# Halo copies at even steps, a quarter's squares on VectorE, and masks two slots later

## The chip, the cores and the metric

The kernel runs on one core of a Trainium2 chip. The time is in device microseconds (us), from the first to the last work of one execution. A kernel's time is the median of several executions on the chip. The core has a matrix engine (TensorE, "PE" in the profile, with its weight loads as "PEld"), a vector engine (VectorE, "DVE"), a scalar engine (ScalarE, "ACT"), a general engine (GpSimd, "POOL") and an engine that here only issues DMAs (SyncE, "SP"). Each takes its instructions in the order in which the program has put them; they wait for each other through semaphores. TensorE writes its products into PSUM banks, and the others read them from there.

## The reference

Four layers on `x` of shape (1024, 16, 16, 16), that is batch, height, width and 16 channels, in float32. Each layer is `x = x + layer(gn(x))`, where `gn` is a group norm over 8 groups of two channels.

```python
def _gn(v, G=8, eps=1e-5):
    g = v.reshape(B_, H_, W_, G, C_ // G)
    m = jnp.mean(g, axis=(1, 2, 4), keepdims=True)
    s = jnp.var(g, axis=(1, 2, 4), keepdims=True)
    return ((g - m) / jnp.sqrt(s + eps)).reshape(v.shape)
...
# layers 1 and 3: a cell update, xt is x with the channels first
    pre = _alive(xt)                       # 3x3 maximum of channel 3 > 0.1
    p = jnp.concatenate([xt, y1, y2], axis=1)   # y1, y2: two 3x3 filters of each channel
    h = jax.nn.relu(flat @ fc0_w.T + fc0_b)     # 48 -> 128, for each position
    d = (h @ fc1_w.T + fc1_b)                   # 128 -> 16
    xn = (xt + d) * (pre & _alive(d))
...
# layer 2: a 3x3 convolution, 16 -> 16 channels
    out = jax.lax.conv_general_dilated(x, filters, (1, 1), 'SAME', ...) + bias
...
x = x + layer0(_gn(x))    # a product with a matrix in tensor-train form
x = x + layer1(_gn(x))    # cell update
x = x + layer2(_gn(x))    # convolution
x = x + layer3(_gn(x))    # cell update
```

## The kernel before

The batch is cut into two chunks of 512, `n` = 0 and 1; the normed input of each lies in SBUF as `X0` and `X1` (128 partitions x 32 lines x 512). While a layer works on one chunk, the other engines prepare the other chunk for the next pass: they load it, norm it, and store it. The unnormed values (`xf`) lie in DRAM.

After layer 0, which ends near 1762 us, there are six passes. This document calls them

- cell pass 1 and 2: layer 1 on chunks 0 and 1 (about 1762 to 2030 and 2030 to 2278 us),
- convolution pass 1 and 2: layer 2 on chunks 0 and 1 (2278 to 2388 and 2388 to 2492),
- cell pass 3 and 4: layer 3 on chunks 0 and 1 (2492 to 2750 and 2750 to 3018); pass 4 also turns the result into the order of the output, and a tail of DMAs ends at 3041.

*The order.* `run()` puts the steps of a pass (`main`) one after the other and weaves other work between them. Each such list `bg` comes with a span `(bg, lo, hi)`, as shares of the pass: a step of `bg` is put behind the main step at which its share is reached. In one engine's queue the order is then fixed; nothing overtakes. In cell pass 1, the work woven in first is `last`, in the span 0 to 0.18: the group norm of the last quarter of chunk 0. Then the norm of the other chunk follows.

*A norm.* For a quarter (`parts_cw`) or a whole chunk (`norm_cw`, `norm_lines`): sums over lines (L614, L622, L630 on VectorE), a matmul for the mean (L749, in `norm_lines` L717), a copy of it to SBUF by ScalarE (L678), the subtraction (L655), squares (L640 on ScalarE, or L642 on VectorE, where `on_act` is not set), the sum of the squares (L622, L630, named `s2`), a matmul for the variance (L753, L721), its root on ScalarE (L695), the reciprocal with a Newton step (L701 to L705), a matmul that spreads it (L765), and the multiplication (L655). Sums and squares have few buffers (`t4`).

*A cell pass* works on quads (four lines) in 64 turns; two quads, `v` = 0 and 1, make a column pair (q, w2), eight pairs make a quarter q. The first layer of the cell's network is a set of tile matmuls (L1495, K of 32 rows, up to four of them side by side), each sum in one of six `h` banks, which ScalarE empties with a ReLU into `hid` (L1498). The second layer, `fc1` (L1346, 8 matmuls in two halves for a pair: one for each `v`), writes `po` in one of two `o` banks. `plan()` fixes the turns beforehand: a slot is one set of tiles or one `fc1`, and there are 241 slots, six to a pair in the first quarter. With the second `fc1` of a pair comes `finish`: in the first quarter a flag of the new value (L1354), and always the update `u` (L1358, two buffers), both on VectorE. A flag of the old value (L1376) is made at a pair's first tile.

*The masks.* They depend on the position in the pair and are made in the first quarter only. The count matmuls of a pair (L1385, `pcnt`, two products, each in one of the same six `h` banks) need the flags of the pair itself and of its two neighbours; so the mask of pair w2-1 is made after pair w2 is finished, and with the quarter's last pair two masks come at once. VectorE turns the counts into a mask (L1390, L1391). Then GpSimd multiplies the update with it and adds the residual (L1397, L1398), and SP stores the result seven slots later (L1400). In pass 4 the store is replaced by `turn` eight slots later: four transposes (L1407) into an `o` bank and two copies out of it by VectorE (L159).

`later` holds what is to come at a slot; `after(n, fn)` puts `fn` n slots behind the present one. The masks of a pair are put three slots behind the second `fc1`. In the last three quarters the masks are there already, and GpSimd's two steps follow the update at once.

*A convolution pass* goes over 16 lines h in pairs. Seven steps make a pair of lines: for each line two steps of inner products (L1222, two matmuls a step), one step with the products across quarters (L1231) for both lines, and a last inner step for each line. An `o` bank is emptied by ScalarE (L1270), and GpSimd issues a DMA that adds it to `xf` in DRAM (L1271). L1231 reads lines that lie in other partitions; they are copied beforehand into `hx` by ScalarE, eight small copies (L1210) for four lines, which stand in the list `pending`. Each step takes one of them off the list, so they go out in the first eight steps after `pending` was filled, which happens every 14 steps.

Of the kernel before, what the change touches and what calls it, by code (L numbers as in the profile page):

```python
# [103 lines left out]
def conv_preact_kernel(ctx: ExitStack, tc: tile.TileContext, a: dict, out: bass.AP):  # L104
# [498 lines left out]
    def line_sum(parts, name, own, dear=False):  # L603

        st = {}

        def first():
            if own:  # L610
                st["t"], st["q"] = parts[0](), parts[1]()
                return add(1)()
            st["t"] = work([P, 2, NB], "t4", name)
            V.tensor_tensor(st["t"], parts[0](), parts[1](), ALU.add)  # L614

        def add(i):
            def go():
                x = st["q"] if own else parts[i]()
                if own and not dear and i + 1 < len(parts):

                    st["q"] = parts[i + 1]()
                V.tensor_tensor(st["t"], st["t"], x, ALU.add)  # L622
                if own and dear and i + 1 < len(parts):
                    st["q"] = parts[i + 1]()

            return go

        def last():
            st["s"] = work([P, NB], "s", name + "s")
            V.tensor_tensor(st["s"], st["t"][:, 0], st["t"][:, 1], ALU.add)  # L630

        x = 1.2 if dear else 0.0
        return st, [(1.2 + 2 * x, first)] + [(1.2 + x, add(i)) for i in range(2, len(parts))] + [(0.8, last)]
# [95 lines left out]
        steps += [5, var, 2, keep] + rstd(st)  # L729
        return steps + by_rows(each(X, 0, NL, lambda: st["r"], ALU.mult))  # L730

    def parts_cw(X, on_act):

        st = {}
        N = defaultdict(list)
        for q in range(4):
            l0 = 8 * q
            parts = [lambda l=l: X[:, l : l + 2] for l in range(l0, l0 + 8, 2)]
            s1, more1 = line_sum(parts, "s1", False)
            s2, more2 = line_sum(squares(X, l0, 8, on_act), "s2", True, not on_act)  # L740
            N["sums"].append(more1)
            N["sq"].append(
                centred(each(X, l0, 8, lambda q=q: st["m", q], ALU.subtract), more2)
            )
            rows = slice(32 * q, 32 * q + 32)

            def mean_q(s1=s1):
                st["p"] = psum([P, NB], "pmean")
                T.matmul(st["p"], gm_cw, s1["s"], start=True, stop=True)  # L749

            def var_q(rows=rows, s2=s2):
                st["v"] = psum([P, NB], "pvar")
                T.matmul(  # L753
                    st["v"][rows], gv_cw.rearrange("p f j -> p (f j)"), s2["s"],
                    start=True, stop=True,
                )

            def keep_q(rows=rows):
                if "ve" not in st:
                    st["ve"] = work([P, NB], "n", "ve")  # L760
                V.tensor_scalar(st["ve"][rows], st["v"][rows], GN_EPS, None, ALU.add)

            def spread_q(rows=rows):
                st["p"] = psum([P, NB], "pr")
                T.matmul(st["p"], sel[rows], st["r"][rows], start=True, stop=True)  # L765

            N["mean"].append(mean_q)
            N["var"].append(var_q)
            N["keep"].append(keep_q)
            N["held"].append(held(st, q))  # L770
            N["spread"].append(spread_q)
            N["mul"].append(each(X, l0, 8, lambda q=q: st["m", q], ALU.mult))
        return st, N
# [416 lines left out]
    def layer_conv(X, n, other):  # L1190

        st = {}
        pending = []

        def halo(k):

            steps = []

            def begin():
                st["h", k] = work([P, 2, 2, NB], "hx", "hx")
                if k == 0:
                    G.memset(st["h", k][0:32, :, 0], 0.0)

            def copy(b, wh):
                ls = [l for l in (4 * k - 1 + b, 4 * k + 1 + b) if 0 <= l < S]
                at = (ls[0] - (4 * k - 1 + b)) // 2
                l0 = 16 * (1 - wh) + ls[0]
                A.copy(  # L1210
                    st["h", k][32 * b : 32 * b + 32, wh, at : at + len(ls)],
                    X[96 * wh : 96 * wh + 32, l0 : l0 + 2 * len(ls) - 1 : 2],
                )

            def piece(b, wh):
                return lambda: ((b, wh) == (0, 0) and begin(), copy(b, wh))

            return [piece(b, wh) for b in range(4) for wh in range(2)]

        def inner(h, y):  # L1220
            for wh in range(2):
                T.matmul(  # L1222
                    st["po", h][wh], conv["fw"][:, y], X[:, 16 * wh + h + y - 1],
                    start=y == max(0, 1 - h), stop=y == min(2, S - h),
                )

        def across(h):
            rows = slice(0, 96 if h >= S - 2 else P)
            for wh in range(2):
                cols = slice(0, 32) if wh else slice(96, 128)  # L1230
                T.matmul(  # L1231
                    st["po", h][wh][cols], conv["hw"][rows, wh, h % 2],
                    st["h", h // 4][rows, wh, h // 2 % 2], start=False, stop=False,
                )

        def first(h):
            if h % 4 == 0 and h + 4 < S:
                pending.extend(halo(h // 4 + 1))
            st["po", h] = [bank([P, NB], "o", "po2") for _ in range(2)]
            inner(h, max(0, 1 - h))  # L1240
            if h % 2 == 0 and h > 0:
                finish(h - 2)

        def middle(h):
            inner(h, 1)
            if h % 2 == 0 and h > 0:
                finish(h - 1)

        def last(h):
            inner(h, min(2, S - h))  # L1250
            if h == S - 1:
                finish(h - 1)
                finish(h)

        def step(*fs):
            def go():
                for f in fs:
                    f()
                if pending:
                    pending.pop(0)()  # L1260

            return go

        def finish(h):

            if h == 0:
                G.tensor_copy(come, other[0:1, NL - 1, 0:1])
            for wh in range(2):
                r = work([P, NB], "r", "conv")
                A.activation(r, st["po", h][wh], AF.Identity, bias=b2)  # L1270
                G.dma_start(rows_wc(xf[2][n], wh, h), r.unsqueeze(1), accum_op=ALU.add)  # L1271

        steps = []
        for h in range(0, S, 2):
            for j in (h, h + 1):
                steps.append(step(lambda j=j: first(j)))
                if 0 < j < S - 1:
                    steps.append(step(lambda j=j: middle(j)))
            steps += [
                step(lambda h=h: across(h), lambda h=h: across(h + 1)),  # L1280
                step(lambda h=h: last(h)), step(lambda h=h: last(h + 1)),
            ]
        return halo(0), steps

    def layer_nca(X, n, l, L, xo=None):


        st = {}
# [63 lines left out]
        def finish(q, w2, po):  # L1352
            if q == 0:
                V.tensor_scalar(  # L1354
                    st["f", w2][64:96], po[96:128], nca["b1"][96:128], ALIVE, ALU.add, ALU.is_gt
                )
            u = st["u", q, w2] = work([P, NB], "u", "u")
            V.scalar_tensor_tensor(u, po, nca["b1"], X[:, 8 * q + w2], ALU.add, ALU.add)  # L1358
            if q > 0:
                residual(q, w2)  # L1360
                return

            ws = range(w2 - 1 if w2 else 0, 8 if w2 == 7 else w2)

            def masked():
                for w in ws:
                    mask(w)
                    residual(0, w)

            for w in ws:  # L1370
                fetch(w)
            after(3, masked)

        def flags(w2):
            f = st["f", w2] = work([P, NB], "f", "flags", BF16)
# [166 lines left out]
    X0, X1 = XN  # L1542
# [18 lines left out]
    with ExitStack() as es:  # L1561
# [42 lines left out]
        for i in (2, 3):  # L1604
# [1 line left out]
                steps_of(phases[i]), 415, (), (part_steps(i), 0.05, 0.9),  # L1606
                ([lambda: conv.update(s=conv_weights()), 60, lambda: conv["s"]()] if i == 2 else [0.0], 0.0, 0.5),
            )
        nst, N = parts_cw(X0, True)
        for q in range(4):  # L1610
            bg = alone(N, q - 1) if q else [0.0]
            if q == 3:
# [21 lines left out]
    with ExitStack() as es:  # L1634
        shared[0] = "m"
        stage(es, conv_sb, conv_ps)
        (first0, main0), (first1, main1) = layer_conv(X0, 0, X1), layer_conv(X1, 1, X0)
        bg = norm_lines(X1)

        bg = bg[:-16] + woven(bg[-16:], *[(6 + i, copy) for i, copy in enumerate(first1)])  # L1640
        run((lambda: now(first0), main0), 108, load_wc(X1, xf[2][1]), (bg, 0.09, 1.04), by=0.07)
        run(
            (lambda: None, main1), 108, load_cw(X0, xf[3][0]) + [put(L3)], (norm_cw(X0, True), 0.09, 1.06), by=0.07
        )
    with ExitStack() as es:
        shared[0] = "o"
# [41 lines left out]
```

## Time and profile before

| | |
|---|---|
| time, median of 3 runs | 3043.16 us (3041.85 to 3044.43) |
| the profiled execution | 3042.73 us, span 3041.0 us, mean granted TensorE clock 0.989 |
| TensorE busy in cell pass 1 (1762 to 2030) | 262.50 of 268.00 us, clock 0.99 |
| cell pass 2 (2030 to 2278) | 247.25 of 248.00 us, clock 0.99 |
| convolution pass 1 (2278 to 2388) | 106.54 of 110.00 us, clock 0.98 |
| convolution pass 2 (2388 to 2492) | 99.92 of 104.00 us, clock 1.00 |
| cell pass 3 (2492 to 2750) | 255.68 of 258.00 us, clock 0.99 |
| cell pass 4 (2750 to 3018) | 264.10 of 268.00 us, clock 1.00 |

The span is the time from the first to the last instruction in the trace; the execution's own time is 1.73 us longer. Most of the kernel (up to 1762 us) is layer 0, which the change does not reach except for one argument that is evaluated there. How to read it: in every pass TensorE is busy for nearly all of the time, so what matters are single gaps, and whether TensorE ran at full clock behind them. A groups line of the profile gives the code line, the engine, the operation, the tiles (out<-in), the shape, the count, then the busy time and the mean of one, then the idle time ahead of it and what ended that. A line of the timeline gives the start, the length, the engine, the code line, the operation, the tiles, the shape and the count of instructions taken together; in brackets, the idle time ahead of it and whose end released it.

### The profile page before, as it was taken

The numbers are of one execution on the slowest core, as the hardware profiler recorded it, in microseconds if no ns is written. First come the engines' busy times: TensorE is split into PE (matmuls) and PEld (weight loads), VectorE is DVE, ScalarE is ACT, GpSimd is POOL, SyncE is SP. The second block draws the span as 40 slices with busy tenths as digits, with TensorE's granted clock in tenths as the row PEclk, the third lists the DMA queues.
The fourth block names the chain that finished last, engine by engine and source line by source line (L and its number), as shares of the span: only waits on it lengthen the run. The fifth ranks groups of instructions, "written<-read, shape, count | busy, mean of one in ns | idle before, by whom it ended". The sixth has DMA issues, their size and how long they took to land.

```text
span 3041.0 us, 36525 instructions
## 1 busy us (share of the span) xinstructions
PE 2971.9 (98%) x13690; PEld 1239.6 (41%) x13690; DVE 1761.4 (58%) x2340; ACT 1099.3 (36%) x1806; POOL 671.6 (22%) x729
## 2 busy tenths in 40 slices
PE   7999999999999999999999999999999999999996
PEld 5544334444444444444444433333333333333332
DVE  5354337555554555544555668756977766856432
ACT  4431441000000000000101156666667656666563
POOL 1124670200000000000000015434542224432331
PEclk8999999999999999999999999999999999999998
DMA  8543664533334333332222235436437866343555
GB/s 310 225 126 99 147 150 151 166 109 109 109 109 149 124 109 109 109 102 88 88 88 94 71 131 167 137 119 204 124 121 183 193 109 199 123 127 110 155 158 197
DMA packets 251520, 418.37 MB, mean 138 GB/s; under 512 B 34868, under 2 KB 105064, under 8 KB 248272
## 3 DMA queue, kind: packets, MB, share of 16 engines
q1 hardware_dynamic: 225776, 362.53, 36.6%
q0 software_dynamic: 25376, 53.38, 8.5%
q8 instruction: 108, 1.77, 0.2%
q14 instruction: 68, 0.56, 0.1%
q10 hardware_dynamic: 192, 0.13, 0.0%
HBM read 238.58 MB, written 165.53 MB: 133 GB/s over the span
## 4 chain that ended last, share of the span: by engine, by line
PE 88%; issue 4%; POOL 2%; DVE 2%; DMA 2%; ACT 1%; SPq 0%; POOLq 0%; DVEq 0%; ACTq 0%
PE po L1134 51%; PE ph L1495 20%; PE po L1346 7%; PE pw L1057 3%; PE po L1222 2%; POOL xf L1271 1%; PE L_conv_pe L392 1%; PE ptin L866 1%; DVE bn L860 1%; POOL res L1398 1%; PE ptx L1407 1%; POOL u L1397 1%; PE po L1231 0%; ACT hx L1210 0%; DMA gq<-g_dram 0%
## 5 line engine op out<-in xcount | busy, mean ns | idle before, releaser
L1134 PE MATMUL po<-xn,w 128*128 128x512 f32 x3584 | 1575.6, 596 | 0.8 <-DVE xn L946 0.8
L1134 PEld LDWEIGHTS po<-xn,w 128*128 128x128 f32 x3584 | 670.8, 190 | 839.8 <-issue 820.9
L1498 ACT ACTIVATE hid<-ph,pack 128x512 f32<-128x512 f32 x1024 | 652.7, 686 | 381.5 <-PE ph L1495 271.6
L1170 DVE TENSOR_TENSOR r<-r,po 128x512 f32<-128x512 f32 x576 | 377.9, 684 | 577.5 <-PE po L1134 525.0
L1397 POOL TENSOR_TENSOR u<-u,mask 128x512 f32<-128x512 f32 x124 | 193.9, 1564 | 1820.9 <-DVE mask L1391 1404.2
L1062 ACT COPY w<-pw 128x512 f32<-128x512 f32 (+1 forms) x320 | 150.6, 557 | 1212.1 <-issue 1006.4
L1495 PE MATMUL ph<-xn,wq 32*128 32x512 f32 x3664 | 567.1, 611 | 0.0
L1495 PEld LDWEIGHTS ph<-xn,wq 32*128 32x128 f32 x3664 | 233.3, 184 | 270.0 <-issue 237.6
L1495 PE MATMUL ph<-xn,pack 32*128 32x512 f32 x1288 | 298.8, 625 | 4.9 <-ACT hid L1498 3.0
L1346 PE MATMUL po<-hid,pack 128*32 128x512 f32 x2048 | 281.7, 607 | 0.0
L1075 DVE TENSOR_TENSOR w<-w 128x512 f32<-128x512 f32 x320 | 210.9, 686 | 90.6 <-ACT w L1062 90.6
L655 DVE TENSOR_TENSOR xn<-xn,m 128x1024 f32<-128x1024 f32 x160 | 216.2, 1382 | 45.0 <-ACT m L678 44.8
L1358 DVE SCALAR_TENSOR_TENSOR u<-po,pack,xn 128x512 f32<-128x512 f32 x128 | 95.8, 749 | 203.3 <-PE po L1346 197.0
L1398 POOL TENSOR_TENSOR res<-res,u 128x512 f32<-128x512 f32 x124 | 206.5, 1666 | 9.7
L1222 PE MATMUL po<-xn,convw 128*128 128x512 f32 x368 | 166.2, 604 | 2.9 <-ACT conv L1270 2.9
L1495 PEld LDWEIGHTS ph<-xn,pack 32*128 32x128 f32 x1288 | 115.0, 185 | 104.3 <-issue 63.9
L1170 DVE TENSOR_TENSOR xn<-xn,po 128x512 f32<-128x512 f32 x96 | 64.4, 684 | 123.7 <-PE po L1134 123.3
L1346 PEld LDWEIGHTS po<-hid,pack 128*32 128x32 f32 x2048 | 42.8, 108 | 195.2 <-issue 144.3
L622 DVE TENSOR_TENSOR sq<-sq 128x1024 f32<-128x1024 f32 x78 | 109.8, 1407 | 13.3 <-ACT sq L640 12.6
L1222 PEld LDWEIGHTS po<-xn,convw 128*128 128x128 f32 x368 | 68.7, 191 | 99.7 <-issue 90.4
L404 POOL DMA_DIRECT2D L_conv_wy<-xn x160 | 88.8, 563 | 26.8 <-ACT xn L398 15.6
L1057 PE MATMUL pw<-R,gq 32*128 32x256 f32 (+1 forms) x1280 | 89.3, 384 | 2.9 <-DMA gq<-g_dram 2.8
(166 smaller groups left out, 1769.2 us busy)
## 6 DMA issues: line engine op xcount, KB each, us to landing
xf<-r SPq DMA_DIRECT2D x112, 512.0 KB, 3.8
xn<-xf SPq DMA_DIRECT2D x96, 512.0 KB, 4.9
r<-xf SPq DMA_DIRECT2D x80, 512.0 KB, 4.6
wq<-L_conv_wy SPq DMA_DIRECT2D x192, 192.0 KB, 2.8
res<-xf SPq DMA_DIRECT2D x128, 256.0 KB, 3.2
xf<-res SPq DMA_DIRECT2D x96, 256.0 KB, 2.1
res<-xr SPq DMA_DIRECT2D x256, 64.0 KB, 2.8
xf<-conv POOLq DMA_DIRECT2D x64, 256.0 KB, 5.7
```

The source lines that it names most:

```text
L655: V.tensor_tensor(part, part, m().unsqueeze(1).broadcast_to([P, 2, NB]), op)
L1057: T.matmul(pw[r][:, v], st["g", u][rows, v], st["R"][rows, p % 2, 64 * k0 : 256], start=True, stop=True,)
L1062: A.copy(w[:, k0:4, :, 32 * r : 32 * r + 32].rearrange("p k t (v o) -> p v (k t) o", v=2), pw[r],)
L1075: V.tensor_tensor(w[:, k], w[:, x], w[:, y], ALU.add if sign > 0 else ALU.subtract)
L1134: T.matmul(po, st["w", u][:, matrix, t], x, start=t == 0, stop=t == 3)
L1170: V.tensor_tensor(r[at], r[at], po, ALU.add if sign > 0 else ALU.subtract)
L1222: T.matmul(st["po", h][wh], conv["fw"][:, y], X[:, 16 * wh + h + y - 1], start=y == max(0, 1 - h), stop=y == min(2, S - h),)
L1346: T.matmul(po[32 * j : 32 * j + 32], nca["w1"][:, v], hid[j], start=v == 0, stop=v == 1)
L1397: by.tensor_tensor(u, u, st["m"][:, w2], ALU.mult)
L1398: by.tensor_tensor(r, r, u, ALU.add)
L1495: T.matmul(ph, w, x, start=k == 0, stop=k == len(tiles) - 1)
L1498: A.activation(h, ph, AF.Relu, bias=nca["bt"][:, r : r + 1])
```

## The change

There are four edits.

1. `parts_cw` gets an argument `alone_from`. From this quarter on, squares are made by VectorE (L642) and not by ScalarE (L640), with the order of buffers that goes with it. For chunk 0 ahead of cell pass 1 it is 3: the last quarter's four squares, which stand in `last`.
2. In `layer_conv`, the steps count themselves, and a halo copy is taken off the list only when the count modulo 7 is even: at four steps of seven, so eight copies go out in 14 steps and not in eight.
3. In the cell passes the masks of a pair come five slots behind the second `fc1`, not three. With them move the count matmuls, GpSimd's two steps, and what is put seven or eight slots behind these (stores, in pass 4 transposes). This holds for the first quarter of all four cell passes.
4. In convolution pass 2 the norm of chunk 0 for layer 3 starts at 0.12 of the pass, not at 0.09.

```diff
-    def parts_cw(X, on_act):
+    def parts_cw(X, on_act, alone_from=4):
...
-            s2, more2 = line_sum(squares(X, l0, 8, on_act), "s2", True, not on_act)
+            act = on_act and q < alone_from
+            s2, more2 = line_sum(squares(X, l0, 8, act), "s2", True, not act)
...
                 for f in fs:
                     f()
-                if pending:
+
+                st["n"] = st.get("n", 0) + 1
+                if pending and st["n"] % 7 % 2 == 0:
                     pending.pop(0)()
...
             for w in ws:
                 fetch(w)
-            after(3, masked)
+            after(5, masked)
...
-        nst, N = parts_cw(X0, True)
+        nst, N = parts_cw(X0, True, 3)
...
-            (lambda: None, main1), 108, load_cw(X0, xf[3][0]) + [put(L3)], (norm_cw(X0, True), 0.09, 1.06), by=0.07
+            (lambda: None, main1), 108, load_cw(X0, xf[3][0]) + [put(L3)], (norm_cw(X0, True), 0.12, 1.06), by=0.07
```

## The prediction

> **What bounds the kernel now.** I read the page first, then the windows (busy time and granted clock in stretches), then the timeline of each engine where TensorE is not full, and last the built instruction order of both kernels, which carries no times. The names of passes and steps are those of the section on the kernel.
>
> ```profile
> PE 2971.9 (98%) x13690; PEld 1239.6 (41%) x13690; DVE 1761.4 (58%) x2340; ACT 1099.3 (36%) x1806; POOL 671.6 (22%) x729
> PE 88%; issue 4%; POOL 2%; DVE 2%; DMA 2%; ACT 1%; SPq 0%; POOLq 0%; DVEq 0%; ACTq 0%
> ```
>
> TensorE sets the end: 98% busy and 88% of the chain. What is left over is small and local, so an edit is worth what it does to TensorE's order at one place. Three such places, from the timeline and from windows of 4 us (columns: stretch, length, busy us of PE, PEld, DVE, ACT, POOL, clock, DMA share, GB/s):
>
> ```profile
> 1781.86 1.80 PE L1495 MATMUL ph<-xn,pack 32*128 32x512 f32 x3 [2.96 <-ACT hid L1498]
> ...
> 1784.00:1788.00 4.00, 4.00 (x17) 0.60 (x11) 1.92 (x2) 1.75 (x3) 0.00 (x0) 0.50 0.00 0
> ...
> 2347.70 5.40 PE L1222 MATMUL po<-xn,convw 128*128 128x512 f32 x8 [2.93 <-ACT conv L1270]
> ...
> 2348.00:2352.00 4.00, 4.00 (x6) 1.54 (x6) 2.40 (x3) 3.95 (x6) 2.88 (x4) 0.59 0.73 81
> ...
> 2399.48 1.13 PE L749 MATMUL pmean<-s1s,gm_cw 128*128 128x512 f32 x2 [1.32 <-DVE s1s L630]
> ...
> 2413.99 1.05 PE L753 MATMUL pvar<-s2s,gv_cw 128*32 128x512 f32 x2 [2.76 <-DVE s2s L630]
> ```
>
> The reader is to see that a stall of 3 us is followed by a stretch at half the clock: a busy TensorE there does half its work. The whole mask cycle of one column pair, in cell pass 3, where VectorE has nothing else to do:
>
> ```profile
> 2518.59 1.06 PE L1346 MATMUL po<-hid,pack 128*32 128x512 f32 x8
> 2519.58 0.39 PE L1385 MATMUL pcnt<-flags,alive_w 32*128 32x512 bf16 x2
> ...
> 2520.14 2.84 PE L1495 MATMUL ph<-xn,pack 32*128 32x512 f32 x15
> 2522.90 1.07 PE L1346 MATMUL po<-hid,pack 128*32 128x512 f32 x8
> ...
> 2520.44 0.69 DVE L1390 TENSOR_SCALAR mask<-pcnt 128x512 bf16<-128x512 f32 x1 [1.59 <-PE pcnt L1385]
> 2521.24 0.69 DVE L1391 SCALAR_TENSOR_TENSOR mask<-pcnt,mask 128x512 bf16<-128x512 f32 x1
> ...
> 2524.91 0.75 DVE L1358 SCALAR_TENSOR_TENSOR u<-po,pack,xn 128x512 f32<-128x512 f32 x1
> ...
> 2522.01 1.16 POOL L1397 TENSOR_TENSOR u<-u,mask 128x512 f32<-128x512 f32 x1 [4.96 <-DVE mask L1391]
> 2523.25 1.26 POOL L1398 TENSOR_TENSOR res<-res,u 128x512 f32<-128x512 f32 x1
> ```
>
> Call the start of the count matmuls (L1385, 2519.58) P. The masks are done at P+2.35, GpSimd has read `u` at P+4.93 and the next update (L1358) starts at P+5.33, 0.40 after it could: with two `u` buffers it must wait for GpSimd, and the margin is 0.4 us.
>
> **What the Trainium skill says.** "TensorE: Matmul & The Clock Gate", "What's actually happening": the array falls to half clock after an idle window of about 3.4 us, free-running, and recovers after a busy one. The trace agrees: 0.50 and 0.59 behind the two stalls above, none behind the 2.76 one. "GPSIMD Engine Reference", "8. Key points": GpSimd shares its SBUF interfaces with VectorE instructions that read two SBUF operands. It agrees: L1397 takes 1.16 alone and 2.07 to 2.14 beside the L622 sums (2551.00, 2089.91). "Perfetto Trace Analysis", "Optimization Strategy": a gap that repeats can mean too few buffers; the waits of `u` are of that kind.
>
> **The change part by part.** The sum is made against the profiled execution: span 3041.0, execution 3042.73, which is 0.43 under the median 3043.16.
>
> *Squares of the last quarter (cell pass 1).* Off ScalarE: four L640 of 1.05 to 1.07, 4.2 us. Onto VectorE: four L642, at the 1.14 pitch that chained 128x1024 ops show there (1778.92 to 1780.06). What it can win: the first two L1354 stand 13.57 us apart (1774.66, 1788.23), in cell pass 3 6.76 apart (2502.87, 2509.63), so at most 6.8: the ScalarE stall and the half clock behind it. What replaces it: by the new order VectorE runs from 1773.40 three subtractions, four squares, three sums and the fourth subtraction (11 x 1.14 = 12.5), two flags 1.52, two updates 1.50, L1376 0.42 and L630 0.69, in sum 16.6, so s2s comes at 1790.0, not at 1786.46. The variance matmul (L753), which stands in TensorE's queue with tiles, counts and L1346 behind it, waits for it; with ScalarE free TensorE gets there near 1784 and idles some 6 us, long enough for the half clock. So the stall moves from ScalarE to VectorE. Behind it the reciprocal (3.35) and the flags of the fourth pair come some 2 us later than 1806.61, and the count matmuls wait for those flags already now (0.97 at 1807.43). I take +2; bounds -5 (stall and clock gone) and +6 (VectorE's 3.5 us lateness goes through whole).
>
> *Halo copies (both convolution passes).* Nothing is added: the same L1210 copies (1.04 each), popped at four steps of seven and not at the first eight. The last copy still leaves four steps before its L1231. Stall at 2347.70: between two evacuations ScalarE ran eleven ops, 2335.58 to 2346.96; now five squares and three copies stand there. But a square waits for VectorE's two ops, 2.27 per square, so the fourteenth ends near 2345.0, not 2346.30, and the evacuation starts near 2346.1: 0.9 won, and with a stall of 2 the clock (0.59 over 4 us, 1.6) probably holds. I take -2; bounds -4.5 (2.93 + 1.6) and +2 (a copy held behind squares makes L1231 late). GpSimd's adds to DRAM keep their order.
>
> *0.09 to 0.12 in convolution pass 2.* L749 and the first L753 move two L1222 later, 2 x 0.89 = 1.77. The 1.32 wait goes. The 2.76 wait shrinks to about 1, but the fourth square now stands behind an evacuation and a copy (some 0.9 late). I take -1.3; bounds -4.1 (both gone) and +2 (the denser normalisation comes late at the end).
>
> *Masks two slots later (four cell passes).* What moves: count matmuls, L1390, L1391, L1397, L1398; with them on SP the stores L1400, two slots later past `res` and `wq` loads; in pass 4 the transposes L1407 and their copies L159. The counts now stand directly before the second L1346 of the pair. Queued behind the update that waits for GpSimd are L1376, the normalisation and the next masks; TensorE waits for these through the banks. Passes 2 and 3: update at P+4.97, end P+5.72, 2.3 us later than now relative to its matmul, but its `po` bank is due only a pair later. The second and third tile behind the counts take the count banks, free at P+2.4; from there 1.93 for tiles, 1.0 for L1346 and 1.93 for the next tiles give P+7.26, and now the period is 7.25: the stretch of 2.84 behind the counts merely changes its cause. I take 0 per period. The double mask at the quarter's end stalls both ways; L1346 now covers 1 us, VectorE is 3 us later (2557.73 to about 2560.8) and the clock may dip again: together +1.3 for the two, bounds -3 and +5.
>
> Pass 4 differs: the transposes take `o` banks (two), so the first L1346 of a pair takes the bank of the pair before and waits for its update. Now it just fits:
>
> ```profile
> 2784.47 0.75 DVE L1358 SCALAR_TENSOR_TENSOR u<-po,pack,xn 128x512 f32<-128x512 f32 x1
> ...
> 2785.40 1.07 PE L1346 MATMUL po<-hid,pack 128*32 128x512 f32 x8
> ```
>
> The bank is free at 2785.22 and taken at 2785.40. After: free at P+5.78; then 1.0 and 1.93 to the next P, a period of 8.71 against 7.83 (2782.47 to 2790.30), five times 0.88 = 4.4. Some 1 us comes back where L1346 covers the double mask; a clock dip may cost 1.7. I take +4; bounds 0 and +9. The tail after it is unchanged, 23 us from the last L1407 to the end.
>
> Sum: 2 - 2 - 1.3 + 1.3 + 4 = +4.0; 3042.73 + 4.0 = 3046.7.
>
> **The rivals.** *Slower: the stretch does not change its cause but doubles.* Where VectorE carries other work (passes 1 and 4), the masks start late and tiles behind the counts wait for them on top of ScalarE's banks: 0.84 (2.77 less 1.93) in six periods of two passes, 10.1 more: 3057. For it: L1376, subtractions and transposes stand between update and mask. Against: VectorE is idle during GpSimd's 2.5 us. It decides once the tiles behind counts take over 3.6 us.
>
> *Faster: the stalls go and the new waits hide.* 2.93 + 1.6 in convolution pass 1 and 1.32 + 2.76 in pass 2 are 8.6, and pass 4 loses nothing: 3034. For it: these stalls are real and TensorE's. Against: squares run at VectorE's pace, and pass 4 has 0.2 us of margin. It ends on the other side of before, and decides if the update in pass 4 finishes before TensorE is through the tiles.
>
> *No effect at all*: masks and squares only move, 3043; it is the upper end of the faster case and the lower of mine.
>
> **How the numbers follow.** About 0.2% (6 us) is what a measurement of this kernel can tell from no change: under 3037.1 is faster, over 3049.2 slower. My case has 0.56, own range 3041 to 3053: 0.32 of it the same, 0.24 slower, since the upper bounds of its terms reach further than the lower ones. The slower rival has 0.26, all slower. The faster one with the no-effect edge has 0.18: 0.11 faster, 0.07 the same. So faster 0.11, same 0.39, slower 0.50. The range, 3036 to 3058, takes in mine, most of the faster one and about half of the slower.
>
> **What would show it.** Right: L753 near 1790 with a PE wait on DVE s2s of several us and a clock under 0.7 behind it; the wait at the second L1222 group of convolution pass 1 under 2 us; no 1.32 wait for L749; in pass 4 a wait of L1346 for DVE u L1358 of about 0.9 in each pair, and period 8.7; in passes 2 and 3 a period of 7.2 to 7.3. Wrong: periods over 7.6 in passes 2 and 3 (slower rival), or pass 4 still at 7.8 (faster one).

## The result, and the profile after

| | before | after | ratio, 95% interval |
|---|---|---|---|
| median over 20 runs each | 3044.4 us (3040.77 to 3048.66) | 3048.64 us (3043.14 to 6100.67) | 1.0014 (1.0008 to 1.002) |
| a second set, 13 runs of after, 19 of before | 3045.71 us (3039.9 to 3050.56) | 3045.9 us (3040.68 to 3052.45) | 1.0004 (0.9996 to 1.0012) |
| the profiled execution shown here | 3042.73 us, span 3041.0 | 3043.14 us, span 3041.4 | |

One run of after in the first set took 6100.67 us, double the others, and is left out of the ratio; the median of the other 19 is 3048.36. The change costs a few microseconds: 4.3 (2.4 to 6.1) by the first set, 1.2 (1.2 less to 3.7 more) by the second, which by itself does not tell it from no change. The two profiled executions differ by only 0.4, and they hide large terms of both signs. Whole times also scatter ahead of the change: cell pass 1 starts between 1760.24 and 1765.36 us in the profiles below, though layer 0 has the same code in all. So the useful view is the length of each pass, read from TensorE's timeline: from the first matmul of a pass to the first of the next, convolution pass 1 to the first L1231 of convolution pass 2, and cell pass 4 to the start of its last four transposes. All in us; the kernels below the first three rows are the experiments.

| profile of | cell 1 | cell 2 | conv 1 | conv 2 | cell 3 | cell 4 |
|---|---|---|---|---|---|---|
| before | 268.74 | 247.43 | 108.80 | 104.85 | 258.99 | 265.36 |
| after | 273.98 | 244.02 | 106.28 | 105.82 | 254.86 | 269.70 |
| after, second profile | 273.93 | 244.02 | 106.28 | 108.85 | 254.88 | 269.70 |
| squares | 271.55 | 246.32 | 107.11 | 104.79 | 259.28 | 265.21 |
| masks | 273.72 | 244.03 | 107.11 | 107.58 | 254.87 | 269.87 |
| halo | 268.83 | 245.97 | 107.94 | 105.16 | 259.04 | 265.21 |
| late | 268.74 | 247.42 | 108.81 | 105.51 | 258.78 | 265.22 |
| masks_mid | 268.77 | 244.02 | 108.81 | 105.38 | 254.88 | 265.20 |
| mid_halo | 268.65 | 244.02 | 107.99 | 105.18 | 254.87 | 265.37 |
| u3_only | 267.90 | 245.62 | 107.10 | 105.69 | 258.63 | 265.19 |
| masks_u3 | 269.94 | 243.51 | 108.80 | 105.55 | 254.82 | 265.00 |
| after_u3 | 269.05 | 243.50 | 107.98 | 105.54 | 254.80 | 265.00 |

Each row is one execution. Where the code is the same, cell passes 1 and 4 and convolution pass 1 repeat to 0.2 us (cell pass 4 at three slots: 265.19 to 265.37), cell passes 2 and 3 to about 0.6; convolution pass 2 scatters by 0.9 (104.79 to 105.69). On top of that come jumps of about 1.7 in single passes, which are the clock; they are explained at the end. After against before, the change adds 5.2 in cell pass 1 and 4.4 in cell pass 4 and saves 3.4 and 4.1 in cell passes 2 and 3. The page has little of this. Its busy times and its chain:

```profile
PE 2964.5 (97%) x13690; PEld 1235.5 (41%) x13690; DVE 1762.8 (58%) x2344; ACT 1096.6 (36%) x1802; POOL 665.8 (22%) x729
PE 90%; DVE 3%; issue 3%; DMA 1%; ACT 1%; POOL 1%; SPq 0%; DVEq 0%; POOLq 0%; ACTq 0%
```

TensorE is as full as before and bounds the kernel as before; the four squares show in the counts of VectorE (2340 to 2344) and ScalarE (1806 to 1802). In this kernel the lines from L749 to L1231 have numbers 2 higher, and those from L1270 on 4 higher: L753 is L755, L1346 is L1350, L1358 is L1362, L1398 is L1402.

*Cell pass 1.* From the timeline of TensorE, then windows of 4 us (stretch, length, busy us of PE, PEld, DVE, ACT, POOL, clock, DMA share, GB/s):

```profile
1790.18 1.89 PE L755 MATMUL pvar<-s2s,gv_cw 128*32 128x512 f32 x2 [6.15 <-DVE s2s L630]
...
1811.52 0.37 PE L1389 MATMUL pcnt<-flags,alive_w 32*128 32x512 bf16 x1 [1.05 <-DVE flags L1358]
...
1817.74 1.07 PE L1350 MATMUL po<-hid,pack 128*32 128x512 f32 x8 [1.47 <-DVE u L1362]
```

```profile
1786.00:1790.00 4.00, 0.00 (x0) 0.00 (x0) 3.92 (x5) 0.00 (x0) 0.00 (x0) 0.77 0.72 237
1790.00:1794.00 4.00, 3.82 (x14) 1.19 (x18) 0.45 (x2) 0.00 (x0) 0.00 (x0) 0.50 0.46 175
...
1818.00:1822.00 4.00, 4.00 (x24) 1.33 (x18) 0.04 (x1) 2.43 (x4) 0.00 (x0) 0.61 0.94 269
```

The stall that was ScalarE's (2.96 before) is VectorE's, 6.15 us long, and ends at 1790.18; the reading of 0.00 for TensorE with 3.92 for VectorE is the handover. A second stall with a stretch at 0.61 follows it, and its releaser is the update `u`: that L1362 starts at 1816.84, after 1.82 us of waiting for GpSimd, and L1350 needs it because the matmul that spreads the reciprocal (L767, at 1812.82) has taken one of the two `o` banks.

*Cell pass 4.* TensorE, VectorE and GpSimd in one period, from their timelines:

```profile
2785.12 1.05 PE L1389 MATMUL pcnt<-flags,alive_w 32*128 32x512 bf16 x6
...
2790.97 1.06 PE L1350 MATMUL po<-hid,pack 128*32 128x512 f32 x8 [0.67 <-DVE u L1362]
```

```profile
2790.07 0.75 DVE L1362 SCALAR_TENSOR_TENSOR u<-po,pack,xn 128x512 f32<-128x512 f32 x1 [1.83 <-POOL res L1402]
```

```profile
2787.54 1.16 POOL L1401 TENSOR_TENSOR u<-u,mask 128x512 f32<-128x512 f32 x1 [6.19 <-DVE mask L1395]
2788.77 1.27 POOL L1402 TENSOR_TENSOR res<-res,u 128x512 f32<-128x512 f32 x1
```

Read from the bottom: GpSimd is done with an old `u` at 2790.04, the update starts at 2790.07 after 1.83 of waiting, ends at 2790.82, and the first `fc1` of the pair, which needs its `o` bank, starts 0.15 later, having waited 0.67. The counts start at 2785.12 and next at 2793.81, a period of 8.69.

*The end of the quarter in cell pass 3*, first before, then after, in windows of 4 us:

```profile
2556.00:2560.00 4.00, 2.65 (x18) 0.78 (x16) 3.78 (x7) 0.69 (x1) 0.70 (x1) 0.94 0.73 212
2560.00:2564.00 4.00, 4.00 (x25) 1.33 (x18) 1.75 (x2) 2.29 (x4) 3.91 (x3) 0.64 0.27 79
```

```profile
2556.00:2560.00 4.00, 4.00 (x30) 1.16 (x23) 3.92 (x5) 2.42 (x4) 0.01 (x1) 1.00 0.94 316
2560.00:2564.00 4.00, 4.00 (x30) 1.89 (x28) 2.56 (x5) 1.43 (x3) 2.65 (x3) 1.00 0.34 121
```

Where TensorE stood for 1.3 of 4 us and then ran at 0.64, it is full and at full clock. Its timeline after:

```profile
2556.95 2.25 PE L1389 MATMUL pcnt<-flags,alive_w 32*128 32x512 bf16 x10
2559.13 1.07 PE L1350 MATMUL po<-hid,pack 128*32 128x512 f32 x8
2560.13 1.13 PE L751 MATMUL pmean<-s1s,gm_cw 128*128 128x512 f32 x2
2561.18 0.69 PE L1499 MATMUL ph<-xn,pack 32*128 32x512 f32 x1
```

The masks of this place come later than before (VectorE starts the first at 2559.70, before at 2557.73), but `fc1` and the mean matmul now stand behind the counts and give TensorE 2.05 us of work while VectorE makes the masks.

*The convolution passes.* In pass 1 the wait for the evacuation is 2.11 after 2.93, with no stretch under full clock. In pass 2 the 1.32 wait of L749 is gone in this profile (in the second one it is there, 1.23), the wait of the first variance is not, and small ones are new:

```profile
2409.50 1.98 PE L1224 MATMUL po<-xn,convw 128*128 128x512 f32 x4 [0.36 <-ACT conv L1274]
2414.28 1.05 PE L755 MATMUL pvar<-s2s,gv_cw 128*32 128x512 f32 x2 [2.79 <-DVE s2s L630]
2428.97 1.04 PE L755 MATMUL pvar<-s2s,gv_cw 128*32 128x512 f32 x2 [0.25 <-DVE s2s L630]
2446.61 0.62 PE L755 MATMUL pvar<-s2s,gv_cw 128*32 128x512 f32 x1 [0.62 <-DVE s2s L630]
2456.20 1.98 PE L1224 MATMUL po<-xn,convw 128*128 128x512 f32 x4 [0.61 <-ACT conv L1274]
```

VectorE's first sum for this norm, before and after, waits for a load:

```profile
2394.68 1.22 DVE L614 TENSOR_TENSOR s<-xn 128x1024 f32<-128x1024 f32 x1 [9.69 <-DMA xn<-xf]
```

```profile
2394.22 1.23 DVE L614 TENSOR_TENSOR s<-xn 128x1024 f32<-128x1024 f32 x1 [9.73 <-DMA xn<-xf]
```

The pass starts at 2387.47 and 2386.97, so the sum starts 7.2 us into it both times. The edit moves TensorE's place for the mean, not the sums.

### The profile page after: what moved, and what is told of

The parts are those of the page before. It is cut to its first block, busy times and chain, and to the rows that moved or that the text cites. A ratio compares the mean times of both kernels' runs of the same rounds, so it can differ in the third digit from the quotient of the medians.

```text
span 3041.4 us, 36532 instructions
## 1 busy us (share of the span) xinstructions
PE 2964.5 (97%) x13690; PEld 1235.5 (41%) x13690; DVE 1762.8 (58%) x2344; ACT 1096.6 (36%) x1802; POOL 665.8 (22%) x729
## 3 DMA queue, kind: packets, MB, share of 16 engines
q8 instruction: 108, 1.77, 0.2%
## 4 chain that ended last, share of the span: by engine, by line
PE 90%; DVE 3%; issue 3%; DMA 1%; ACT 1%; POOL 1%; SPq 0%; DVEq 0%; POOLq 0%; ACTq 0%
PE po L1136 51%; PE ph L1499 21%; PE po L1350 8%; PE po L1224 3%; PE pw L1059 3%; PE L_conv_pe L392 1%; PE ptin L868 1%; PE po L1233 1%; DVE sq L622 1%; DVE bn L862 1%; PE pcnt L1389 1%; POOL res L1402 1%; PE pr L767 0%; PE ptx L1411 0%; POOL u L1401 0%
## 5 line engine op out<-in xcount | busy, mean ns | idle before, releaser
L1350 PE MATMUL po<-hid,pack 128*32 128x512 f32 x2048 | 279.3, 604 | 6.4 <-DVE u L1362 6.4
L1499 PE MATMUL ph<-xn,pack 32*128 32x512 f32 x1288 | 275.2, 626 | 1.0 <-DVE xn L1172 0.8
L655 DVE TENSOR_TENSOR xn<-xn,m 128x1024 f32<-128x1024 f32 x160 | 217.6, 1391 | 40.3 <-ACT m L678 40.1
L1362 DVE SCALAR_TENSOR_TENSOR u<-po,pack,xn 128x512 f32<-128x512 f32 x128 | 95.8, 749 | 230.6 <-PE po L1350 184.6
L1402 POOL TENSOR_TENSOR res<-res,u 128x512 f32<-128x512 f32 x124 | 203.7, 1643 | 9.7
L1499 PEld LDWEIGHTS ph<-xn,pack 32*128 32x128 f32 x1288 | 105.9, 186 | 108.9 <-issue 87.2
L1350 PEld LDWEIGHTS po<-hid,pack 128*32 128x32 f32 x2048 | 42.6, 108 | 194.0 <-issue 141.7
L622 DVE TENSOR_TENSOR sq<-sq 128x1024 f32<-128x1024 f32 x78 | 109.8, 1407 | 12.6 <-ACT sq L640 11.7
L642 DVE TENSOR_TENSOR sq<-xn 128x1024 f32<-128x1024 f32 x52 | 91.9, 1783 | 1.1
```

Of the source, the lines that this page charges most:

```text
L655: V.tensor_tensor(part, part, m().unsqueeze(1).broadcast_to([P, 2, NB]), op)
L1350: T.matmul(po[32 * j : 32 * j + 32], nca["w1"][:, v], hid[j], start=v == 0, stop=v == 1)
L1402: by.tensor_tensor(r, r, u, ALU.add)
L1499: T.matmul(ph, w, x, start=k == 0, stop=k == len(tiles) - 1)
```

## The experiments

The profile after shows what each pass gained or lost, but not which edit did it: two edits share cell pass 1, and two share convolution pass 2. So each edit was first made alone.

### Each edit alone

**squares**: edit 1 alone.

```diff
-        nst, N = parts_cw(X0, True)
+        nst, N = parts_cw(X0, True, 3)
```

> Edit 1 alone: the four squares of the last quarter on VectorE, all else as before. Pass 1 took 268.7 us before and 274.0 with all four edits; the other passes must stay within 1 us of before. Theory A (as predicted: the stall only moves from ScalarE to VectorE): L753 waits about 6 us for s2s, pass 1 takes 270 to 271.5, the time rises by about 2 us (ratio 1.0007). Rival B (the squares are the whole loss of pass 1): pass 1 takes 273 to 275, the time rises by 5 us (1.0017). Rival C (the ScalarE stall and its half clock go and nothing replaces them): pass 1 under 266, time 3 us down (0.999).

Measured: ratio 1.0003 (0.9995 to 1.0011), which by itself cannot tell the theories apart. The profile can: cell pass 1 took 271.55, 2.8 more than before, just above theory A's range; B and C fall. The wait splits in two, because here the count matmuls stand ahead of the variance (in this kernel the lines concerned have numbers 1 higher than before):

```profile
1790.83 0.58 PE L1386 MATMUL pcnt<-flags,alive_w 32*128 32x512 bf16 x1 [4.16 <-DVE flags L1355]
...
1792.31 1.89 PE L754 MATMUL pvar<-s2s,gv_cw 128*32 128x512 f32 x2 [0.90 <-DVE s2s L630]
```

Both wait for VectorE, which works off the squares. Of the 2.8, TensorE standing still is 2.5 (7.54 us in the pass against 5.00), and half clock some 1.3, since this profile has 10.24 us of half clock in the pass and before 6.83; the matmuls themselves take about 1 less. The other passes were to stay within 1 us; cell pass 2 (1.1 less) and convolution pass 1 (1.7 less), whose code is unchanged, did not. Before has one stretch of half clock in each of these two passes, squares none; see the end.

**masks**: edit 3 alone.

```diff
-            after(3, masked)
+            after(5, masked)
```

> Edit 3 alone: masks five slots behind in all four cell passes, squares left on ScalarE. Theory A (effects are local and add up): pass 1 about 271.5 (3 us more than before, from updates that wait 1.6 us for GpSimd's u), pass 2 about 244 and pass 3 about 255 (3.4 and 4.1 less: the double mask's stall and its half clock window go), pass 4 about 270.5 (4.3 more, period 8.7); sum near 0, ratio 1.000. Rival B (pass 1's loss is the squares' alone): pass 1 unchanged at 268.7, time 3 us down, ratio 0.999. Rival C (the gain of passes 2 and 3 in the one profile is a half clock window that other executions don't have): passes 2 and 3 gain 1.7 each or less over many executions, time 3 to 4 us up, ratio 1.0012.

Measured: ratio 1.0003 (0.9994 to 1.0011). Passes 2, 3 and 4 came as theory A had them (244.03, 254.87, 269.87). Cell pass 1 took 273.72: the masks alone cost 5.0 there, nearly as much as all four edits together (5.2). So B falls, and the size in A was too small. The two edits do not add in this pass, 2.8 and 5.0 giving 5.2. What does not add is mainly the clock: by standing still squares alone add 2.5, masks alone 2.0 and all four edits 5.1, but masks alone have 13.65 us of half clock in the pass, squares and after 10.24, before 6.83. Where the masks alone lose it, in TensorE's timeline:

```profile
1808.26 2.03 PE L1495 MATMUL ph<-xn,pack 32*128 32x512 f32 x3 [2.73 <-DVE mask L1390]
...
1821.89 1.07 PE L1346 MATMUL po<-hid,pack 128*32 128x512 f32 x8 [1.03 <-DVE u L1358]
```

The first is a mask that VectorE makes at 1807.51, right behind the norm's reciprocal chain of 1801.51 to 1807.48; the tiles behind the counts wait for its bank. The second is the update behind GpSimd. Convolution pass 2 (107.58), whose code is unchanged, has a half-clock stretch that before has not. As to theory C, the gain of passes 2 and 3 is too regular to be chance: see masks_mid.

**halo**: edit 2 alone.

```diff
+                st["n"] = st.get("n", 0) + 1
-                if pending:
+                if pending and st["n"] % 7 % 2 == 0:
```

> Edit 2 alone: halo copies at four steps of seven. Theory A: convolution pass 1 about 106.3 us against 108.8 (the wait for the evacuation goes from 2.93 to about 2.1 and its half clock window goes), convolution pass 2 within 0.5 of before (104.9); time 2.5 us down, ratio 0.9992. Rival B (what is won in pass 1 is lost in convolution pass 2, where copies now stand between squares and evacuations): convolution pass 2 about 1 us longer, with new waits of L1222 for ACT conv; time 1 to 1.5 us down, ratio 0.9996.

Measured: ratio 0.9995 (0.9987 to 1.0004), convolution pass 1 107.94, pass 2 105.16. The pass 1 figure meets neither theory: it still has a half-clock stretch. Compared like with like the gain is 0.82 or 0.83: with such a stretch 108.80 becomes 107.98 (after_u3), without it 107.11 (squares) becomes 106.28 (after). That is the stall's own shortening, 2.93 to 2.11 or 2.12. Pass 2 shows no waits that before had not, so B's loss is not there.

**late**: edit 4 alone.

```diff
-(norm_cw(X0, True), 0.09, 1.06)
+(norm_cw(X0, True), 0.12, 1.06)
```

> Edit 4 alone: the norm in convolution pass 2 starts at 0.12. Theory A (as predicted): the 1.32 us wait of L749 goes and the 2.76 us wait of L753 shrinks to about 1 to 1.5, convolution pass 2 takes 102 to 103.6 against 104.9; ratio 0.9996. Rival B (the chain of sums and squares only starts later, so L753 still waits some 2.8 us and the later variances wait too): convolution pass 2 takes 105 to 106, ratio 1.0002.

Measured: ratio 1.0 (0.9992 to 1.0008), convolution pass 2 105.51. Theory B fits: L749 no longer waits, but the first variance waits 2.53 and the later groups 0.51, 0.39 and 0.60. The first sum still starts with the load (9.47 us of waiting), so s1s is as early as before; TensorE, which no longer waits for it at the mean, waits at the first variance instead. Over all profiles without a half-clock stretch in this pass the mean is 105.62 with edit 4 (after, late, after_u3) and 105.23 without (before, squares, halo, masks_mid, mid_halo, u3_only, masks_u3): 0.4 more, inside the scatter of 104.79 to 105.69.

### The masks where they help, and a third buffer where they hurt

**masks_mid** moves them in cell passes 2 and 3 alone, **mid_halo** adds edit 2:

```diff
-            after(3, masked)
+            after(5 if (n == 1) != (l == 3) else 3, masked)
```

> Edit 3 in passes 2 and 3 alone; passes 1 and 4 keep three slots. Theory A (local effects): pass 1 268.7, pass 2 244.0, pass 3 254.9, pass 4 265.3; against before 2 to 3.4 us less in pass 2 (how much depends on where the half clock window fell before) and 4.1 in pass 3, so 5.5 to 7.5 us less in all, ratio 0.9975 to 0.9985. Rival B (the gain of the single profiles doesn't last over many executions): ratio 0.9993 or above.

> Edit 3 in passes 2 and 3 alone, and the halo copies of edit 2; squares and the start at 0.09 as before. Theory A: what masks_mid wins and 0.8 us (no half clock window in convolution pass 1 either way) to 2.5 us (the window goes) more: ratio 0.997 to 0.998, the fastest of all. Rival B (the shorter stall of 2.1 us catches a window as often as that of 2.9, and the squares of convolution pass 2 lose what pass 1 wins): no faster than masks_mid.

Measured: masks_mid 0.9971 (0.9959 to 0.9982), 3036.23 us; mid_halo 0.9965 (0.9953 to 0.9978), 3034.34 us, beside 3045.71 for before. They ran 6 and 5 times, and both ratios lie a little below theory A's ranges, with intervals that reach into them. Passes 2 and 3 took 244.02 and 254.88, and in all seven profiles of the table with masks five slots behind these two passes lie at 243.5 to 244.0 and 254.8 to 254.9. The gain lasts, so theory B, and theory C of the masks, fall. Whether mid_halo is faster than masks_mid the intervals do not tell; its convolution pass 1 is 0.82 shorter.

**masks_u3** is edit 3 with a third buffer for `u`; to make room the tiles `wq` have four and not five.

```diff
-            after(3, masked)
+            after(5, masked)
...
-    nca_sb = dict(t4=2, s=3, n=2, wq=5, mask=1, f=5, hid=8, u=2, r=4, nx=1)
+    nca_sb = dict(t4=2, s=3, n=2, wq=4, mask=1, f=5, hid=8, u=3, r=4, nx=1)
```

> Edit 3 alone, with a third update buffer (u=3; to make room the weight tiles wq have four buffers and not five). With the masks alone pass 1 took 273.7 us and pass 4 269.9, against 268.7 and 265.4 before. Theory A (the update that waits for GpSimd's u is what both passes pay for): the update starts as soon as its matmul is done, pass 4's wait of L1346 for DVE u (0.67 a period, 2.27 at the end) is gone and pass 4 takes 265 us or less; in pass 1 the waits of 1.6 to 1.9 us of L1358 go, and it takes 270 to 272, what is left being the masks behind the reciprocal (the 2.73 us wait for mask L1390); passes 2 and 3 stay at 244 and 255. Time 4 to 6 us down against before, ratio 0.998 to 0.9987. Rival B (the wait for GpSimd was only where the lateness showed; with it gone the tiles behind the counts or the transposes wait for something else): pass 4 stays within 1.5 us of 269.9 and pass 1 within 1 us of 273.7; ratio 1.000 or above.

Measured: ratio 0.997 (0.9959 to 0.9982). Cell pass 4 is back at 265.00, as theory A had it, and cell pass 1 at 269.94, just below its range; the time is below its range too, since u=3 brings something of its own (u3_only). The group of updates in cell pass 4 (2750 to 2825 us; busy, mean ns | idle before, what ended it), first in masks, then in masks_u3:

```profile
L1358 DVE SCALAR_TENSOR_TENSOR u<-po,pack,xn 128x512 f32<-128x512 f32 x9 | 6.7, 749 | 11.1 <-POOL res L1398 11.0
```

```profile
L1358 DVE SCALAR_TENSOR_TENSOR u<-po,pack,xn 128x512 f32<-128x512 f32 x9 | 6.7, 749 | 0.3
```

11.0 us of waiting for GpSimd are gone, and with them 4.9 of the pass. `wq=4` was not run without `u=3`; the other kernel with both (u3_only, below) changes this pass by no more than 0.2. In cell pass 1 the mask behind the reciprocal still makes TensorE wait (1.79), and 1.2 of the 5.0 stay.

**u3_only** and **after_u3**: the same buffers with none and with all of the four edits, so this one line on the kernel before and on the kernel after.

```diff
-    nca_sb = dict(t4=2, s=3, n=2, wq=5, mask=1, f=5, hid=8, u=2, r=4, nx=1)
+    nca_sb = dict(t4=2, s=3, n=2, wq=4, mask=1, f=5, hid=8, u=3, r=4, nx=1)
```

> The buffers of masks_u3 (u=3, wq=4) without any of the four edits: masks three slots behind, as before. Theory A (with masks at three slots the update has at most 0.4 us to wait, so the third buffer wins nothing without the move): passes 1 to 4 within 0.5 us of before (268.7, 246.0 to 247.4, 259.0, 265.3), ratio 0.9993 to 1.0007. Rival B (the third buffer is itself the gain of masks_u3): pass 2 near 244, pass 3 near 255, ratio 0.998 or below.

> All four edits and the third update buffer (u=3, wq=4). Theory A (the wait for u is what makes the change cost time): pass 4 at 265.0 against 269.7, pass 2 at 243.5 and pass 3 at 254.8, pass 1 at 270 to 272 against 274.0, convolution passes as in the kernel after; 7 to 9 us below the kernel after, ratio to before 0.997 to 0.9985. Rival B (with the squares on VectorE pass 1 is bound by VectorE's order, not by u): pass 1 stays at 273.5 or above; ratio 0.9985 to 0.9995.

Measured: u3_only 0.9989 (0.9981 to 0.9997), after_u3 0.9974 (0.9965 to 0.9983). The buffer alone is worth a little: neither theory of u3_only is right, cell pass 1 is 0.8 shorter. The waits of 0.33 to 0.38 us that the update has for GpSimd there in before are gone in u3_only, and so are two waits of TensorE for a mask behind them, 0.32 and 0.42 us, which is nearly all of the 0.8. But passes 2 and 3 (245.62, 258.63) are not those of masks_u3, so its gain there is the masks'. In after_u3 every cell pass improves on the kernel after, pass 1 by 4.9, below the range that theory A gave; the 6.15 wait for s2s is still there and the 1.47 wait for `u` is not, nor the half clock behind it (6.83 us in the pass against 10.24, some 1.7 of the 4.9). With one more buffer the kernel with the change is 0.26% faster than before.

**after_again**: the kernel after, a second time.

> The kernel after the change once more, on this chip beside the others, for a second profiled execution. Theory A (the passes repeat; the executions differ only by where half clock windows fall): pass 1 273 to 275.5, pass 2 and 3 at 244.0 and 254.9 to 0.3, pass 4 269.7 to 0.3, convolution pass 1 95.7 or 97.4; ratio 1.0005 to 1.002. Rival B (other stalls come and go from run to run): passes 2 to 4 differ by more than 1 us from the first profile.

Theory A fits cell passes 1 to 4 (273.93, 244.02, 254.88, 269.70). The lengths that it gives for convolution pass 1, 95.7 or 97.4, are not lengths of this table; the pass repeats (106.28 both times). The ratio, 1.0004, is just below its range. Convolution pass 2 took 3.0 more than in the first profile, which neither theory had as such. Of this, 1.23 is a wait of L751 for s1s that the first profile lacks: a sum waits 1.84 for a load (with the start at 0.09 this wait is in every profile, 1.10 to 2.46). Another 1.7 is one half-clock stretch of 3.41 us behind the wait for s2s.

## Why the prediction was right in its sum, and where not

The forecast was +4.0 us, and the larger set measured +4.3 (2.4 to 6.1), the smaller +1.2 (1.2 less to 3.7 more). By the profiles, with means over all kernels whose pass has the same code, the change is 5.2 - 2.8 - 0.8 + 0.4 - 4.1 + 4.4 = +2.3 for the six passes in order. So the total was right, and that was in good part luck, because terms that were wrong offset each other; the masks in cell passes 2 and 3 alone were off by 8. By the prediction's own mark of 6 us the result is "the same", to which it gave 0.39; it gave "slower" 0.50. The terms:

| step of the prediction | taken | measured |
|---|---|---|
| squares, cell pass 1 | +2 | +2.8 alone |
| masks, cell pass 1 | 0 | +2.4 more (5.2 less 2.8); +5.0 alone |
| halo copies | -2 | -0.8 |
| 0.09 to 0.12 | -1.3 | +0.4 |
| masks, cell passes 2 and 3 | +1.3 | -6.9 (-2.8 and -4.1) |
| masks, cell pass 4 | +4 | +4.4 |

- *Squares*: the mechanism was right, to the number. s2s was put at 1790.0, and it ends at 1790.03; an idle time of some 6 us was 6.15; the half clock behind it came. The hit on 1790.0 is in part luck: VectorE started at 1772.69, not 1773.40, and took 17.3 for the 16.6 summed. The size was 0.8 short by one profile, less than the 1.7 that one half-clock window more or less makes.
- *Cell pass 4*: right in mechanism and size: a wait of L1350 for the update (0.67 for the forecast 0.9), a period of 8.69 for 8.71, and masks_u3 shows that the two `u` buffers are its cause.
- *Masks in cell pass 1*: taken at nothing, without a reason of its own. The update there waits 1.8 us for GpSimd as in pass 4, and reaches TensorE where the spread matmul takes an `o` bank, which the prediction had seen only of pass 4's transposes. And this was the mechanism of the slower rival, at that pass alone: masks behind VectorE's other work make the tiles wait (2.73 in masks), with half clock behind it.
- *Masks in cell passes 2 and 3*: the step that failed is "the double mask at the quarter's end stalls both ways", with a half clock that "may dip again". The masks do come later, but the work now behind the counts covers them, so stall and half clock go. Pass 3's 4.1 comes apart so: TensorE stands still 1.35 less (2.32 to 0.97, with the old stall's 1.03 and 0.22 in it), a half-clock stretch of 3.41 us, worth 1.7, is gone, and the remaining 1.1 lies in the periods. The six from the first counts to the last take 40.3 for 41.6: the steady period, 7.25 before, was forecast at 7.26 and is 7.15, and the last one is 6.80 for 7.36.
- *Halo copies*: the step that was mis-sized is the clock. The wait was forecast 0.9 shorter and is 0.82 shorter (2.11, so the sign "under 2 us" was just missed), but half clock followed the stall of 2.1 in three of five profiles, and that of 2.9 in four of seven. That a shorter stall keeps the clock up more often is not shown.
- *0.12*: the step that failed is "the 2.76 wait shrinks to about 1"; it is 2.79. By the prediction the two L1222 ahead of the variance bring TensorE there 1.77 later, but the 1.32 that it no longer waits at the mean brings it there earlier again: it reaches L755 24.5 us into the pass, L753 before at 23.8. And s2s is 0.8 later too (27.25 for 26.46), since a sum waits 0.94 for the fourth square, which the prediction had as 0.9. The two waits are for one chain that starts with a load, so taking the first away lengthens the second.

The faster rival's case did not come: the convolution's stalls are shorter by 0.8 or stay, and pass 4 does lose. The stalls that went are those of the double masks, which it had not named. (Of the prediction's "2.07 to 2.14" for L1397 beside the L622 sums, 2.07 is L1397 and 2.14 is L1398.)

## What to carry to other kernels

Before moving a consumer back in a rotating schedule, count the buffers of what it consumes: here two more slots on a two-buffer tile made each update wait 1.8 us for GpSimd, and a third buffer gave nearly all of the time back (4.9 us in one pass, 3.8 of 5.0 in the other). Ask at each place that the move reaches what stands behind the moved work afterwards; the same edit saved 2.8 and 4.1 us in two passes, where other matmuls then covered a wait, and cost 5.0 and 4.4 in two others. And when a sum comes out right, look at the terms pass by pass before trusting the model behind it.

## What was unexpected of the hardware

The same stall in the same code costs different amounts in different executions, because the clock may or may not drop behind it. Convolution pass 1 is 108.80 long with the drop and 107.11 without, both with the same wait of 2.93 us: 1.69 us, which at half clock is a stretch of 3.4 us.

The clock records of the traces show what decides. In before, half clock starts in the six passes at 1781.24, 2098.68, 2347.86 and 2559.48, which is 93, 73 and 62 times 3.413 us apart, and lasts one or two such windows; the other traces have the same grid, each with its own start. "TensorE: Matmul & The Clock Gate" of the Trainium skill, "What's actually happening", gives a window of 3413 ns that runs free of the kernel, and this agrees. The stall of 2.93 in windows of this grid, first before, then squares:

```profile
2344.44:2347.86 3.42, 0.49 (x2) 0.16 (x2) 3.42 (x4) 3.35 (x5) 0.00 (x0) 1.00 0.01 2
2347.86:2351.27 3.41, 3.41 (x5) 1.34 (x6) 2.54 (x3) 3.36 (x6) 2.21 (x3) 0.50 0.61 71
```

```profile
2346.64:2350.05 3.41, 2.13 (x5) 0.58 (x4) 3.41 (x4) 3.34 (x4) 0.00 (x0) 1.00 0.01 2
2350.05:2353.47 3.42, 1.76 (x4) 0.86 (x5) 3.13 (x3) 3.32 (x6) 1.52 (x2) 1.00 0.15 7
2353.47:2356.88 3.41, 3.41 (x13) 0.95 (x11) 2.02 (x2) 2.58 (x4) 1.99 (x3) 1.00 0.96 132
```

In before the whole stall falls into one window (TensorE busy for 0.49), and the next runs at half clock. In squares it is split, 1.28 and 1.65, and the clock stays at 1.00. This sorts the convolution passes of all twelve profiles: nine windows in which TensorE stood still for 2.06 us or more were each followed by half clock, and none with 1.92 or less was. It also sorts the wait for s2s in the two profiles of the kernel after: 2.79, split into 1.43 and 1.48 with a short wait ahead of it, had no drop, and 2.80 within one window had one.

So the stall needn't be as long as the window, and the prediction's "The trace agrees" goes too far: its two stalls of 2.96 and 2.93 us are shorter than the 3.4 us that it names, and its 2.76 was spared because it was split (1.49 and 1.28). In the cell passes 2 us is not the mark: in before, 0.75 us of standing still in a window was followed by half clock in cell pass 2, and 1.65 in cell pass 4 of masks was not; what decides there stays open. For a comparison of two profiles this means that a difference of 1.7 us in one pass is no evidence of anything until the half-clock windows in both have been counted.
